# A planner's order of instructions, and a region that keeps it

## Chip, core and metric

The kernel runs on one core of one Trainium2 chip. A core has a matrix engine (TensorE; PE for its matmuls, PEld for its weight loads), a vector engine (VectorE, DVE), a scalar engine (ScalarE, ACT), a general engine (GpSimd, POOL) and SyncE (SP), which issues the DMAs here. Each engine takes its instructions from a list of its own and waits on semaphores for what others make. The metric is the device time of one execution in microseconds (us); less is better.

## What is computed

Four graph layers run over 16 graphs of 1024 nodes with 128 features. Cut to what matters:

```
x = layernorm(x + relu((mask^T x) U / deg))                       # layer 0: sum over neighbours
x = layernorm(x + softmax(clip(q k^T * adj) - 9e15*(1-adj)) v)    # layer 1: attention, q, k, v = relu(x W + b)
x = layernorm(x + concat_h softmax_i(leaky(s_i + s_j)) (x W)_h)   # layer 2: four heads, masked by adj
x = layernorm(x + sage3(x, dilate(adj)))                          # layer 3: three sage layers on thinned edges
```

`dilate` walks the rows of a graph and drops every n-th neighbour of a row, and earlier drops change later rows; the kernel replaces the walk by two rounds of thresholds and counts.

## The kernel before

Two stages follow one another. `fuse` (L181) computes layers 0 to 2 and the dilation for all graphs; `sage` (L1070) computes layer 3. The change touches the last statement of `fuse` alone.

In `fuse` a graph is a batch `b`. The work of a batch is cut into ten generators, called sequences: `loads` (the rows of adj come by DMA), `signs` (`has` on DVE at L332, `over` on ACT at L336), `dilate`, `layer0`, `layer1`, `scores`, `values`, `sides`, `layer2` and `layer2_sums`. Each yields a `Step` before the instructions that it issues: the engine, a cost in us that the planner books, the marks that it waits for, and the buffers that it takes and gives back.

`Loom.run` (L163) is a planner that runs while the program is being made. It keeps a clock for each engine from the booked costs. Over and over it takes the step that can start first, and among those of the same engine that can start within 0.1 us of it the one that is due first by a table of phases; it books that step and lets its sequence emit the instructions. So the order in which the kernel emits its instructions, over all engines, is the order of planned start. For every hand-over from one engine to another it books 0.3 us, and 0.5 us when the receiver is PE.

What the planner computes is not yet the order on the engines. The framework that builds the program has a scheduler of its own. It uses the order of emission as priorities, runs its own model of time, and lets an instruction pass an earlier one on the same engine when the earlier one is not ready in that model. The instructions of the built program carry running numbers in the order of emission, and they can be set against the trace: in the ten batches between 591.2 and 2076.0 us, 1101 of 3001 DVE instructions, 717 of 1664 ACT instructions and 1146 of 11732 matmuls ran ahead of one on their engine that had been emitted earlier.

Steps that the prediction follows, in the order of emission within a batch:

- `stays` (L537): 16 blocks of nine matmuls into `ps_n` (L541, L544, L547), two PSUM buffers; each is emptied by ACT into `adt` (L557). The last block is the last reader of the tile `ranked`, which has one buffer.
- norm 2 and norm 0 (`Norm.apply`, L576): 17 small DVE instructions on the tile `ln_t` (L582 to L594), nearly each reading the one before, then eight on ACT (L599). The planner books 1.9 us for the DVE part.
- the scans (L354): eight DVE instructions that fill `ranked` of the next batch, booked at 2.2 us each.
- `weights`: `top` (L879, DVE), `ps_top` (L882, PE), `peak` and `peaks` (L885, L887, DVE), `ps_cap` (L890, PE), `cap` (L896, DVE), `ac` (L899, DVE; L903, L904, ACT), `wh` (L893, ACT).
- `pieces`: `src` (L917, L921, DVE), then three parts of it rounded in turn on ACT (L924, L930) and DVE (L927, L933).
- `ps_m` (L968, PE): 192 matmuls that read `pieces`; `every` (L973, ACT) empties it.
- `sides`: `sg` (L818, ACT, 32 a batch) and `g` (L827, DVE), which the matmuls `ps_b` (L998) read.
- `values`: transposes (L605, PE), `pt` (L772, ACT), `ps_a` (L779, PE). `ps_s` of the scores is L744 and L748.

Of the kernel before, what the change touches and what calls it, by code (L numbers as in the profile page):

```python
# [180 lines left out]
def fuse(S, ctx, a, x3, adt_d, viol, B=16):  # L181
# [20 lines left out]
    tc, nc = S.tc, S.nc  # L202
# [111 lines left out]
    def signs(batches):  # L314

        for k, c in enumerate(batches):
            yield k, "signs"
            again = k == len(batches) - 1
            if k >= 2:
                yield Step(  # L320
                    None, 0.0, after=(f"m {k - 2} 1", f"sides {k - 2}") + ((f"dilated {k - 2}",) if k > 2 else ())
                )
            links[c] = p2.tile([P, 8, EDGE + N], F8, name="has")
            V.memset(links[c][:, :, EDGE - 2 : EDGE].bitcast(I16), 0)
            has[c] = links[c][:, :, EDGE:]
            for r in range(8):
                yield Step(
                    "DVE", 0.64, after=(f"a {k} {r}",), give=[("a", r)] if again else (),
                    mark=f"has {k} {r}",
                )  # L330
                t = raw.pop((k, r))
                V.tensor_scalar(has[c][:, r, :], t, 0.0, LINK, ALU.not_equal, ALU.mult, saturate=False)  # L332
                if not again:
                    yield Step("ACT", 1.13, after=(f"a {k} {r}",), take=[("over", (k, r))], give=[("a", r)])
                    over[c, r] = p2.tile([P, N], F8, name="over", bufs=OVER)
                    nc.scalar.activation(  # L336
                        over[c, r], t, AF.Sign, bias=under, accum_out=cut[:, c, r : r + 1], saturate=False
                    )
# [351 lines left out]
    def layer1():  # L690
        for b in each:
            yield b, "keys"
            yield Step(None, 0.0, after=(f"x1 {b} 1",) + ((f"early {b - 1}",) if b else ()))
            yield from keys(b)
# [35 lines left out]
    def scores():  # L730
        for b in each:
            yield b, "scores"
            yield Step(None, 0.0, after=(f"q {b}", f"k {b}"))
            qt, kt, _ = qkv[b]
            low = lows[b] = sm.tile([P, 8], F32, name="low")
            for ib in range(8):
                for f in range(0, N, 512):
                    yield Step(
                        "PE", 1.07, after=(), take=() if f else [("two", "s"), ("pr", ib)],
                        give=[("over", (b, ib))] if f else (),  # L740
                    )
                    if f == 0:
                        ps_s = two.tile([P, N], F32, name="ps_s", tag="two")
                    nc.tensor.matmul(  # L744
                        ps_s[:, f : f + 512], qt[:, ib * P : (ib + 1) * P], kt[:, f : f + 512],
                        start=True, stop=False,
                    )
                    nc.tensor.matmul(  # L748
                        ps_s[:, f : f + 512], shut, over[b, ib][:, f : f + 512], start=False, stop=True
                    )  # L750
                yield Step("DVE", 1.15)
                V.tensor_reduce(low[:, ib : ib + 1], ps_s, AX.X, ALU.min)  # L752
                yield Step("ACT", 1.1, give=[("two", "s")], mark=f"pr {b} {ib}")
                pr, tot = p2.tile([P, N], F32, name="pr"), sm.tile([P, 1], F32, name="tot")
                nc.scalar.activation(pr, ps_s, AF.Exp, bias=low[:, ib : ib + 1], scale=-1.0, accum_out=tot)  # L755
                made[b, ib] = pr, tot
# [46 lines left out]
    def sides():  # L803

        for b in range(B):
            yield b, "sides"
            for h in range(H):
                for q in range(4):
                    for k in range(2):
                        yield Step(  # L810
                            "ACT", 1.04, after=(f"row {b} {h}", f"st {b}"),
                            take=[("g", (b, h, q // 2))] if k == 0 and q % 2 == 0 else (), mark=f"sg {b} {h} {q}",
                        )
                        st, side = stuff[b][0:2]
                        if k == 0:
                            sg = p2.tile([P, 2, N], I8, name="sg")
                        ib = 2 * q + k
                        nc.scalar.activation(  # L818
                            sg[:, k, :], rows[b, h], AF.Sign, bias=st[:, 1, h, ib : ib + 1], scale=-1.0
                        )  # L820
                    if q == 3 and h + 2 < H:
                        yield Step("SP", 0.2, lag=2.5, mark=f"row {b} {h + 2}")
                        row(b, h + 2)
                    yield Step("DVE", 0.6, after=(f"sg {b} {h} {q}",), mark=f"g {b} {h} {q // 2}" if q % 2 else None)
                    if q % 2 == 0:
                        side[h, q // 2] = p4.tile([P, 4, N], F8, name="g")
                    V.tensor_tensor(  # L827
                        side[h, q // 2][:, q % 2 * 2 : q % 2 * 2 + 2, :].bitcast(I16), sg.bitcast(I16),
                        has[b][:, 2 * q : 2 * q + 2, :].bitcast(I16), ALU.bitwise_and,
                    )  # L830
            yield Step(None, 0.0, mark=f"sides {b}")

    def layer2():
        for b in each:
            yield b, "weights"
            yield Step(None, 0.0, after=(f"x2 {b} 1",) + ((f"raw wh {b - 1}", f"sides {b - 1}") if b else ()))
            yield from weights(b)
# [110 lines left out]
    def layer2_sums():  # L948
        for b in each:
            yield b, "sums"  # L950
            yield from outputs(b)

    def outputs(b):
# [73 lines left out]
        for c in range(8):  # L1027
# [7 lines left out]
    loom = Loom(  # L1035
        155.0, 0.1,
        {
            "loads": (364.0, 3.34),
            "signs": (813.0, 0.64),
            "ranks": (991.0, 0.88),  # L1040
            "match": (-250.0, 0.22),
            "round 0": (-892.0, 0.48),
            "round 1": (-332.0, 0.32),
# [17 lines left out]
        },  # L1061
        two=2, one=2, dps=2, g=4, pr=2, a=2, w2k=4, over=OVER,
    )
    loom.run(
        layer2_sums(), sides(), values(), layer2(), scores(), layer1(), layer0(), signs(batches),
        loads(batches), dilate(batches),
    )
# [292 lines left out]
def tile_gnn_stack(tc, a, out):  # L1360

    nc = tc.nc
    with ExitStack() as outer:
        flag = outer.enter_context(tc.tile_pool(name="flag", bufs=1))
        viol = flag.tile([P, 8], F32, name="viol")
        nc.vector.memset(viol, 0.0)
        with ExitStack() as ctx:  # L1370
            S = Setup(ctx, tc)
            dram = ctx.enter_context(tc.tile_pool(name="fast_dram", bufs=1, space=DRAM))
            x3 = dram.tile([16, 8 * P, P], F32, name="x3")
            adt_d = dram.tile([16, 8, P, 8 * P], F8, name="adt_d")
            with ExitStack() as first:
                fuse(S, first, a, x3, adt_d, viol)
            with ExitStack() as third:
                layers = [[a[f"L3_gnn_{n}{i}"] for n in ("Wr", "Wx", "b", "g", "be")] for i in (1, 2, 3)]
                sage(S, third, x3, a["nodemask"], adt_d, viol, layers, a["L3_gnn_Wl"], a["L3_gnn_bl"], out)
            todo = flag.tile([1, 1], I32, name="todo")  # L1380
            with tc.tile_pool(name="flag_ps", bufs=1, space=PSUM) as fp:
                ps = fp.tile([1, 8], F32, name="ps_flag")
                nc.tensor.matmul(ps, S.ones[:, 0:1], viol, start=True, stop=True)
                total = flag.tile([1, 1], F32, name="total")
                nc.vector.tensor_reduce(total, ps, mybir.AxisListType.X, ALU.max)
                nc.vector.tensor_copy(todo, total)
        v = nc.values_load(todo[0:1, 0:1], min_val=0, max_val=16384)  # L1387
        with tc.If(v > 0):
            general(tc, a, out)
# [676 lines left out]
```

## Time and profile before

| what | us |
|---|---|
| median of 3 runs | 3487.2 (3486.0 to 3496.1) |
| the profiled execution, as timed | 3491.4 |
| its span, first to last instruction | 3489.7 |
| PE busy in the span | 3010.6 (86%) |
| DVE busy | 2595.9 (74%) |
| ACT busy | 2323.7 (67%) |
| x3 stores of batches 2 and 12 issued at | 591.2 and 2076.0 |

The profile gives the busy time of each engine, groups of equal instructions, and the idle time before them with what ended it. `L998 PE ps_b` stands for line 998, engine PE, output tile `ps_b`. The stores of x3 are the end of a batch in `fuse`: ten batches lie between 591.2 and 2076.0 us, so a batch takes 148.5 us. `fuse` ends at about 2461 us, where the last x3 is stored; the rest is `sage`. In the ten batches PE is busy for 1308.7 us, ACT for 1190.8 and DVE for 1125.5.

### The profile page before, as it was taken

Reading aid. Unit: us, or ns where it says so; the run is one execution under the profiler, and the core shown is the slowest. Engines: PE = TensorE matmul, PEld = TensorE weight load, DVE = VectorE, ACT = ScalarE, POOL = GpSimd, SP = SyncE. Lnnn points to the kernel's source line nnn. Section 1 sums busy time; section 2 is a strip of 40 time slices with the busy share of each in tenths; the row PEclk is TensorE's granted clock in tenths of the full one; section 3 lists DMA queues with packets and bytes.
Section 4 is the critical chain, followed back from the end, with each engine's and each line's share of the span. In section 5 each row is a group of like instructions: output and inputs, shape, how many; then the busy total and the mean of one; then the engine's idle time right before and its main releaser. Section 6 shows DMA issues by size and latency. Waiting matters only on the chain. (4 is left out here: it accounts for less than half of the span.)

```text
span 3489.7 us, 66022 instructions
## 1 busy us (share of the span) xinstructions
PE 3010.6 (86%) x25972; PEld 2377.9 (68%) x25972; DVE 2595.9 (74%) x7057; ACT 2323.7 (67%) x4149; POOL 2.0 (0%) x10
## 2 busy tenths in 40 slices
PE   4897988989898898988989889896599899989974
PEld 3676777777777777767777777775366666666653
DVE  4657687777868778687776868768388788888865
ACT  3786878878778787787878878777355444433334
POOL 0000000000000000000000000000000000000000
PEclk8898989989999999999989999998799999999987
DMA  4121112021120211202111120211333222212224
GB/s 109 37 67 37 61 44 92 25 80 51 48 86 25 80 56 50 77 22 92 49 56 57 42 92 25 74 42 39 76 101 91 73 61 61 61 49 61 61 88 122
DMA packets 224447, 219.97 MB, mean 63 GB/s; under 512 B 48000, under 2 KB 198528, under 8 KB 224128
## 3 DMA queue, kind: packets, MB, share of 16 engines
q1 hardware_dynamic: 224128, 215.67, 20.1%
q8 instruction: 205, 3.36, 0.4%
q14 instruction: 114, 0.93, 0.1%
HBM read 181.80 MB, written 33.82 MB: 62 GB/s over the span
## 5 line engine op out<-in xcount | busy, mean ns | idle before, releaser
L818 ACT ACTIVATE sg<-row,st 128x1024 int8<-128x1024 f32 x512 | 564.0, 1141 | 75.0 <-DVE g L827 55.7
L1165 PE MATMUL ps_g<-pz,ad 128*128 128x384 bf16 (+1 forms) x3072 | 535.8, 327 | 4.6 <-DMA ad<-adt_d 4.4
L1165 PEld LDWEIGHTS <-ad 128*128 128x128 fp8e4 x3072 | 297.6, 98 | 203.8 <-DMA ad<-adt_d 16.6
L998 PE MATMUL ps_b<-pieces,g 128*128 128x198 bf16 x4096 | 392.9, 249 | 3.8 <-DVE g L827 3.1
L998 PEld LDWEIGHTS <-g 128*128 128x128 fp8e4 x4096 | 354.6, 96 | 9.9 <-DVE g L827 4.6
L1182 ACT ACTIVATE sq<-xw 128x128 f32<-128x128 f32 x384 | 117.7, 307 | 305.7 <-DVE xw L1175 272.2
L779 PE MATMUL ps_a<-vn,pt 128*128 128x128 f32 x2048 | 272.7, 283 | 32.6 <-ACT pt L772 32.6
L426 ACT ACTIVATE x<-both,thr 128x1024 f16<-128x1024 bf16 (+7 forms) x384 | 276.1, 769 | 31.6 <-DVE thr L412 22.7
L744 PE MATMUL ps_s<-kt,qt 128*128 128x512 f32 x512 | 276.4, 622 | 24.0 <-ACT pr L755 14.5
L354 DVE TENSOR_TENSOR_SCAN ranked<-has 128x1024 bf16<-128x1024 fp8e4 x128 | 286.8, 2272 | 12.0 <-PE ps_n L547 11.9
L968 PE MATMUL ps_m<-pieces,has 128*128 128x132 bf16 x3072 | 224.7, 240 | 75.4 <-ACT pieces L930 45.0
L779 PEld LDWEIGHTS ps_a<-vn,pt 128*128 128x128 f32 x2048 | 248.6, 193 | 52.5 <-ACT pt L772 40.0
L968 PEld LDWEIGHTS <-has 128*128 128x128 fp8e4 x3072 | 217.7, 106 | 84.8 <-issue 84.4
L656 PE MATMUL ps_g<-py,has 128*128 128x128 bf16 (+1 forms) x3072 | 227.4, 241 | 35.8 <-DVE cap L896 30.6
L656 PEld LDWEIGHTS <-has 128*128 128x128 fp8e4 x3072 | 215.7, 109 | 37.5 <-issue 32.1
L557 ACT ACTIVATE adt<-ps_n 128x512 fp8e4<-128x512 f32 x256 | 146.5, 592 | 101.8 <-PE ps_n L547 92.8
L1174 DVE TENSOR_REDUCE t<-ps_g 128x128 f32<-128x384 f32 x384 | 206.2, 546 | 6.4 <-PE ps_g L1165 6.2
L1121 PE MATMUL ps_z<-wzx,raw 128*128 128x256 f32 x768 | 192.1, 393 | 10.7 <-ACT raw L1196 3.9
L752 DVE TENSOR_REDUCE low<-ps_s 128x1 f32<-128x1024 f32 x128 | 156.3, 1221 | 52.5 <-PE ps_s L748 48.5
L827 DVE TENSOR_TENSOR g<-sg,has 128x1024 int16<-128x1024 int16 x256 | 173.4, 679 | 28.4 <-ACT sg L818 27.5
L336 ACT ACTIVATE over<-a,under 128x1024 fp8e4<-128x1024 f32 x128 | 147.3, 1151 | 50.4 <-DMA a<-in_adj_dram 43.0
L1121 PEld LDWEIGHTS ps_z<-wzx,raw 128*128 128x128 f32 x768 | 144.1, 195 | 45.9 <-PE ps_y L1142 13.6
(255 smaller groups left out, 5928.8 us busy)
## 6 DMA issues: line engine op xcount, KB each, us to landing
a<-in_adj_dram SPq DMA_DIRECT2D x136, 512.0 KB, 3.7
ad<-adt_d SPq DMA_DIRECT2D x384, 128.0 KB, 2.3
row<-t_d SPq DMA_DIRECT2D x64, 512.0 KB, 3.8
adt_d<-adt SPq DMA_DIRECT2D x128, 128.0 KB, 1.7
xn<-x SPq DMA_DIRECT2D x32, 512.0 KB, 4.2
x<-in_x_dram SPq DMA_DIRECT2D x16, 512.0 KB, 5.4
x<-x SPq DMA_DIRECT2D x16, 512.0 KB, 4.2
out_dram<-y SPq DMA_DIRECT2D x16, 512.0 KB, 3.2
```

The source lines that it names most:

```text
L354: V.tensor_tensor_scan(ranked[c][:, r, :], has[c][:, r, :], links[c][:, r, EDGE - 1 : EDGE - 1 + N].bitcast(U8), 0.0, ALU.add, ALU.subtract,)
L426: nc.scalar.activation(x, both[:, at[r] : at[r + 1]], AF.Abs, bias=far[:, r : r + 1], scale=2.0)
L656: nc.tensor.matmul(ps_g[:, k, 0:e], has[b][:, jb, ib * P : (ib + 1) * P], py[:, jb, q * P : q * P + e], start=(jb == 0 and q == 2), stop=( ...
L744: nc.tensor.matmul(ps_s[:, f : f + 512], qt[:, ib * P : (ib + 1) * P], kt[:, f : f + 512], start=True, stop=False,)
L779: nc.tensor.matmul(ps_a[:, 0:P], pt[:, c * P : (c + 1) * P], vn[:, c, :], start=(c == 0), stop=(c == 7))
L818: nc.scalar.activation(sg[:, k, :], rows[b, h], AF.Sign, bias=st[:, 1, h, ib : ib + 1], scale=-1.0)
L827: V.tensor_tensor(side[h, q // 2][:, q % 2 * 2 : q % 2 * 2 + 2, :].bitcast(I16), sg.bitcast(I16), has[b][:, 2 * q : 2 * q + 2, :].bitcast( ...
L968: nc.tensor.matmul(ps_m[:, u // 2, o : o + H * D1], has[b][:, ib, jb * P : (jb + 1) * P], pieces[:, ib, 1, :, t, :], start=(t == 0 and ib ...
L998: nc.tensor.matmul(ps_b[:, u // 2, (u % 2) * 2 * W3 : (u % 2 + 1) * 2 * W3], side[h, q][:, k, jb * P : (jb + 1) * P], pieces[:, 4 * q + k, ...
L1121: nc.tensor.matmul(ps_z[:, k, :], raw[:, b, c * P : (c + 1) * P], wzx, start=True, stop=True)
L1165: nc.tensor.matmul(ps_g[:, 0:width], adt[jb][:, ib * P : (ib + 1) * P], pz[:, jb, 0:width], start=(jb == 0), stop=(jb == 7),)
L1174: nc.vector.tensor_reduce(t, ps_g[:, 0 : 3 * P].rearrange("p (t d) -> p d t", t=3), AX.X, ALU.add)
```

## The change

```diff
-    loom.run(
+    with tc.manual_schedule(): loom.run(
         layer2_sums(), sides(), values(), layer2(), scores(), layer1(), layer0(), signs(batches),
         loads(batches), dilate(batches),
     )
```

Inside the region the framework's scheduler keeps, on each engine and on SP's queue of DMA issues, the order in which the instructions were emitted. No instruction is added or removed, no buffer changes, and the planner's table is as it was. The instructions of `fuse` ahead of the last statement (constants, weights) and all of `sage` are ordered as before.

## The prediction

> **What bounds the kernel.** The change acts in `fuse` alone, so I read the page's 40 slices first: `fuse` fills the first 28, and no engine is full in all of them.
>
> ```profile
> ## 2 busy tenths in 40 slices
> PE   4897988989898898988989889896599899989974
> DVE  4657687777868778687776868768388788888865
> ACT  3786878878778787787878878777355444433334
> ```
>
> PE is the fullest, at eight or nine tenths. The page's chain of waits names only the last ACT instruction, so it says nothing of `fuse`. From the x3 stores ten batches take 1484.8 us, 148.5 each. In them PE is busy for 1308.7 us: 130.9 a batch, so 17.6 us of idle time a batch is all that an order can win. Windows of 10 us through one batch show where that lies (PE, PEld, DVE, ACT, POOL busy with counts, granted clock, DMA share, GB/s).
>
> ```profile
> 1170.00:1180.00 10.00, 9.98 (x132) 8.88 (x130) 8.69 (x38) 6.21 (x14) 0.00 (x0) 1.00 0.16 52
> 1180.00:1190.00 10.00, 9.76 (x142) 8.97 (x139) 5.16 (x7) 8.28 (x18) 0.00 (x0) 1.00 0.62 199
> 1190.00:1200.00 10.00, 2.72 (x31) 2.55 (x29) 10.00 (x11) 6.69 (x8) 0.00 (x0) 0.69 0.19 58
> 1200.00:1210.00 10.00, 5.50 (x50) 5.04 (x49) 10.00 (x24) 8.72 (x12) 0.00 (x0) 0.67 0.15 52
> 1210.00:1220.00 10.00, 10.00 (x137) 10.00 (x136) 10.00 (x29) 5.61 (x8) 0.00 (x0) 0.79 0.01 2
> ```
>
> From 1190 to 1210 PE is idle for 11.8 us and DVE for none; everywhere else in the batch PE has nine tenths or more, but for two windows. So a batch is bound by PE, with one **gap of some 12 us that DVE sets**. The waits of the ten batches agree: PE waits 48.0 us for `peaks`, 23.6 for `cap`, 45.9 for `pieces` (32.5, 9.8 and 3.6), together 11.8 a batch. The rest is small: 24.6 us for `pt`, 10.0 for `pr`, 7.4 for `sums`, 3.8 for `part`.
>
> **What the change moves.** It adds no instruction; every edit is an order. I set the running numbers of emission against the trace and walk one batch.
>
> *What goes.* The framework's scheduler fills the short pauses between dependent DVE instructions with long ones. Norm 0 of this batch, in the DVE timeline:
>
> ```profile
> 1212.37 0.15 DVE L585 TENSOR_TENSOR ln_t<-ln_t 128x8 f32<-128x8 f32 x1
> 1212.44 2.27 DVE L354 TENSOR_TENSOR_SCAN ranked<-has 128x1024 bf16<-128x1024 fp8e4 x1
> 1214.65 0.13 DVE L586 TENSOR_SCALAR ln_t<-ln_t 128x8 f32<-128x8 f32 x1
> 1214.70 2.27 DVE L354 TENSOR_TENSOR_SCAN ranked<-has 128x1024 bf16<-128x1024 fp8e4 x1
> 1216.90 0.13 DVE L588 TENSOR_SCALAR ln_t<-ln_t 128x8 int32<-128x8 int32 x1
> ```
>
> It runs from 1211.28 to 1220.95, 9.7 us; norm 1, which nothing interrupts, takes 3.0 (1163.66 to 1166.69). On ACT whole `sg` of 1.14 us run ahead of `pt`, `pr` and `xt`. What that costs is only what PE waits for: half of the waits for `pt` and `pr` ((24.6 + 10.0)/20 = 1.7 us a batch: one `sg` or less stood in front, and the rest is PE's own transposes or DVE), and those for `sums` and `part`, (7.4 + 3.8)/10 = 1.1. **Gain 2.8 us a batch.** Ends: 0 if each only moves to the next producer, 4.6 if all of it goes.
>
> *What comes, in the gap.* ACT's order in the trace at the `stays`:
>
> ```profile
> 1178.20 1.31 ACT L557 ACTIVATE adt<-ps_n 128x512 fp8e4<-128x512 f32 x2 [1.73 <-PE ps_n L547]
> 1179.93 3.19 ACT L599 ACTIVATE x<-x,ln_t 128x128 f32<-128x128 f32 x8 [0.43 <-DVE ln_t L594]
> ```
>
> The emitted order has four L599 of norm 2, then one L557, four L599, one L557. The planner could put them first because it books 1.9 us for the norm that takes 3.0. In the kept order: the last statistic ends at 1175.4, the norm at 1178.5, four L599 at 0.39 end at 1180.05, and the L557 that ran at 1178.20 ends at 1180.55. Queued behind it on ACT is everything else, and PE's twelfth block of `ps_n` needs the buffer: it starts at 1180.7 and not at 1178.85. The thirteenth waits for the next four L599 and its L557, until 1182.7. Blocks of 0.66 and the 12 `ps_g` between them (0.7 each dozen) bring the last block to 1186.8; in the trace it ended at 1185.9. The scans of the next batch wait for it: 0.9 us later.
>
> Then DVE alone. In the trace, scans start at 1186.02; `peaks` is done at 1195.77, `cap` at 1198.68, `ac` (after one more scan) at 1200.96, and the first half of `pieces` (L933) at 1209.64. Kept order: three scans of 2.2 from 1187.0 to 1193.7; `top` (which ran early, at 1178.0) 1193.9; L671 and two L574, 0.7; a scan, 1196.8; `peak`, `peaks` 1197.2; two `g` and L663, 1.3; a scan, 1200.7; `cap`, `ac`, 1201.0, as in the trace. But `wh` ran early on ACT, at 1191.95; now it is queued behind two `sg` that wait for the `g` at 1197.8, and two L667, so it ends at 1201.4 and the exponentials at 1201.8. `src` takes 2.7 on DVE, to 1204.9; L663 and `g` 0.7; the scan that ran before `ac` now stands here, 2.2; the first L927 half is done at 1208.9, its ACT cast at 1210, L933 at 1212.2. So PE gets `pieces` **2.5 us later**. In the trace PE had also done 8 `ps_t` and 4 `ps_f` (0.61 and 0.70 us by their rows, about 0.9 together without the pipeline's end) that the kept order leaves for later. **Loss 3.4 us a batch**; ends 0, if the walk's waits overlap better, and 6, if the clock adds to it.
>
> Here a rule speaks. PE's timeline in the gap:
>
> ```profile
> 1195.82 0.59 PE L890 MATMUL ps_cap<-peaks,ones 8*128 8x8 f32 x2 [4.95 <-DVE peaks L887]
> 1198.74 5.31 PE L656 MATMUL ps_g<-py,has 128*128 128x129 bf16 x48 [2.33 <-DVE cap L896]
> 1208.39 0.38 PE L968 MATMUL ps_m<-pieces,has 128*128 128x132 bf16 x2 [3.25 <-ACT pieces L930]
> 1209.69 6.48 PE L968 MATMUL ps_m<-pieces,has 128*128 128x132 bf16 x71 [0.92 <-DVE pieces L933]
> ```
>
> 48 matmuls take 5.31 us; in the 1.00 windows a dozen takes 0.7, so they would take 2.8. The Trainium skill (TensorE: Matmul & The Clock Gate, "HAM oscillation") says that a pause longer than about 3.4 us sends the clock to half. The walk cuts the pause of 4.95 into 1.9, 1.3, 2.1, 2.4 and 3.3, so by the rule the clock would stay full, and `ps_m`, half-speed from 1209.7 to 1214, would be 2.0 us shorter: loss 1.4 and not 3.4. By the row the clock is 0.67 in a window in which PE was busy for 5.5 of 10 us with no pause over 3.25. I take the row.
>
> *What comes, elsewhere.* Where PE ran ahead of a matmul that was not ready, the kept order waits. By running numbers that is 2.9 us of matmuls a batch between `values` and the counts (`ps_a` ahead of L452 1.75, L452, L491 and L495 ahead of `ps_a` 0.9, L491 ahead of L452 0.2). A third would be ready sooner without the swaps on ACT and DVE: **loss 1.9 us** (0 to 2.9). On ACT 36 us a batch ran ahead of an unready instruction, 22 of it `sg`; its cover is slack, since the `g` of 1114.52 was read at 1162.59, and ACT has 29.4 us of idle time a batch. On SP the order of the loads, rows and stores returns to emission; `has` still lands ahead of `ps_g` (the last load at about 1167, `ps_g` at 1169): nothing, and up to 2 us if a store of `adt` blocks a load.
>
> **The sum.** 3.4 + 1.9 - 2.8 = 2.5 us a batch, in 15 batches (the first and last are thin and count 0): 37. The profiled execution of 3491.4 becomes 3528; it lies 4.2 above the median, so the median becomes **3524**, 1.1% slower.
>
> **The rivals.**
>
> *Faster, 3420.* One mechanism: norm 2 ends before the L557 are due. If the last `ps_n` ends before 1185.0, the scans start a microsecond earlier instead of later, `pieces` comes at 1209 and the clock stays full. Per batch -0.5 for the gap, -2.0 for the clock, -2.8 for the swaps, +0.8 for unready matmuls: -4.5, times 15 = -67. For it: the planner books scans, `sg` and `g` as the trace spaces them (2.2, 1.04, 0.6), and DVE's swaps are many. Against it: the booked 1.9 for the norm, and a PE that is already nine tenths full outside the gap.
>
> *Much slower, 3612.* ACT becomes the bound. The 36 us that ran ahead find no later place because each head waits (`every` for `ps_m`, `xt` for its transposes, the round's L426 for its thresholds). With 119.1 us busy, ACT bounds the batch once its waits pass 29.4. At 157 us a batch: +8.3 x 15 = +125. Against it: `g` has tens of microseconds of slack.
>
> *No change.* The gains and losses are near each other, or the region binds less than it says: 3487.
>
> **Chances.** A measurement of this kernel can tell 0.3%, about 10 us, from no change. Forecast (3498 to 3570) 0.42; much slower 0.17; faster 0.33; no change 0.08. So slower 0.59, same 0.08, faster 0.33. The range that leaves out two in ten is 3415 to 3630; the forecast's own range is 3498 to 3570.
>
> **What would show it.** DVE: L582 to L594 without a scan between, in about 3 us. ACT: L557 and L599 alternating one to four, and PE waiting for `adt` in `stays` where it had 3.4 us in ten batches. Fewer waits for `pt` and `sums`. The stretch from the last `ps_n` to the first L933, 23.7 us in the trace, near 25. I am wrong if the batch is shorter than 148.5, above all if the granted clock stays at 1.00 through the gap.

## The result, and the profile after

The changed kernel takes **3571.5 us** (median of 4 runs, 3561.7 to 3572.8) against 3486.6 (3478.9 to 3496.1) on the same chip: ratio 1.0236, interval 1.0212 to 1.0259. It is 85 us slower; the forecast was slower by 37. The profiled run took 3572.8 us, its span 3571.1.

One correction to the table ahead of the prediction: 591.2 and 2076.0 are the times at which the x3 stores of batches 2 and 12 landed. They were issued at 586.6 and 2070.2. From here on all stores are counted at their issue (L1032).

| between x3 stores, us | before | after | difference |
|---|---|---|---|
| start to store of batch 2 | 586.6 | 592.0 | +5.4 |
| ten batches, to the store of 12 | 1483.6 | 1522.1 | +38.5 (3.85 a batch) |
| 12 to 13 | 145.7 | 152.4 | +6.7 |
| 13 to 15 | 241.9 | 273.3 | +31.4 |
| the rest, `sage` | 1031.9 | 1031.3 | -0.6 |

So all of it is in `fuse`, and nearly half of it (38 of 82) in the last three batches, to which the forecast gave 5 at most.

In the ten batches PE is busy for 130.8 us a batch, as before (130.7). Nothing was added to its work or to the time that work takes; the whole loss is time in which PE waits. The largest waits of PE in those ten batches, before (us in total, times, longest):

```profile
PE ps_cap L890 <- DVE peaks L887: 48.0, 10, 5.0
PE ps_m L968 <- ACT pieces L930: 32.5, 10, 3.3
PE ps_a L779 <- ACT pt L772: 24.6, 20, 2.5
PE ps_g L656 <- DVE cap L896: 23.6, 10, 2.7
PE ps_m L968 <- DVE pieces L933: 9.8, 10, 1.5
PE ps_n L541 <- ACT adt L557: 3.7, 16, 0.4
```

and after:

```profile
PE ps_m L968 <- ACT pieces L930: 52.6, 10, 5.3
PE ps_n L541 <- ACT adt L557: 35.8, 20, 4.0
PE ps_g L656 <- DVE cap L896: 29.7, 10, 3.1
PE ps_cap L890 <- DVE peaks L887: 24.3, 10, 2.4
PE ps_top L882 <- DVE top L879: 17.8, 10, 1.8
PE ps_m L968 <- DVE pieces L933: 17.8, 10, 1.8
PE ps_a L779 <- ACT pt L772: 10.1, 20, 0.6
PE ps_s L452 <- DVE part L441: 10.0, 20, 0.9
PE ps_s L744 <- ACT pr L755: 6.8, 10, 0.7
```

New is the second row after: 3.6 us a batch for a free `ps_n` buffer (0.4 before). From the first to the last matmul of the `stays` it is now 24.9 us on average where it was 22.2, though 260 matmuls stand in that stretch and not 284. `pieces` has grown from 4.6 to 7.0 a batch, `top` from nothing to 1.8; `peaks` has shrunk from 4.8 to 2.4, `pt` from 2.5 to 1.0. The place in ACT's timeline, for the batch whose gap the prediction walked through:

```profile
1197.38 1.65 ACT L599 ACTIVATE x<-x,ln_t 128x128 f32<-128x128 f32 x4 [2.81 <-DVE ln_t L594]
1198.93 0.57 ACT L557 ACTIVATE adt<-ps_n 128x512 fp8e4<-128x512 f32 x1
1199.40 1.64 ACT L599 ACTIVATE x<-x,ln_t 128x128 f32<-128x128 f32 x4
1200.94 0.58 ACT L557 ACTIVATE adt<-ps_n 128x512 fp8e4<-128x512 f32 x1
```

It is the order of the walk: four L599, one L557, four, one. Ahead of the first, ACT does nothing for 2.81 us, because its head is an L599 whose norm isn't ready; the L557 behind it could have run. PE pays:

```profile
1199.55 0.45 PE L541 MATMUL ps_n<-ranked,less 128*128 128x512 bf16 x1 [2.63 <-ACT adt L557]
...
1201.57 0.58 PE L541 MATMUL ps_n<-ranked,less 128*128 128x512 bf16 x1 [0.72 <-ACT adt L557]
...
1216.98 0.59 PE L890 MATMUL ps_cap<-peaks,ones 8*128 8x8 f32 x2 [2.43 <-DVE peaks L887]
1220.50 4.33 PE L656 MATMUL ps_g<-py,has 128*128 128x129 bf16 x48 [2.92 <-DVE cap L896]
...
1230.17 0.27 PE L968 MATMUL ps_m<-pieces,has 128*128 128x132 bf16 x1 [5.26 <-ACT pieces L930]
```

And the windows of 10 us through this gap (PE, PEld, DVE, ACT, POOL busy with counts, granted clock, DMA share, GB/s):

```profile
1198.00:1208.00 10.00, 7.73 (x96) 6.72 (x96) 2.59 (x6) 6.90 (x16) 0.00 (x0) 0.83 0.39 126
1208.00:1218.00 10.00, 5.37 (x67) 5.02 (x67) 9.93 (x14) 5.21 (x7) 0.00 (x0) 0.94 0.25 88
1218.00:1228.00 10.00, 4.41 (x49) 4.29 (x49) 9.93 (x20) 9.97 (x15) 0.00 (x0) 0.67 0.31 91
1228.00:1238.00 10.00, 6.05 (x60) 5.88 (x60) 8.54 (x29) 2.68 (x4) 0.00 (x0) 0.54 0.05 16
```

In the first window DVE has 2.59 us of work, because its scans wait for the last `ps_n` (38.0 us in ten batches, 4.9 before). In the next two it is full. A stall on ACT has become a pause on DVE just ahead of the stretch that DVE sets.

### The profile page after: what moved, and what is told of

The parts are those of the page before. It is cut to its first block, busy times and chain, and to the rows that moved or that the text cites. A ratio compares the mean times of both kernels' runs of the same rounds, so it can differ in the third digit from the quotient of the medians.

```text
span 3571.1 us, 66293 instructions
## 1 busy us (share of the span) xinstructions
PE 3020.9 (85%) x25972; PEld 2397.1 (67%) x25972; DVE 2657.6 (74%) x7057; ACT 2319.1 (65%) x4149; POOL 2.0 (0%) x10
## 5 line engine op out<-in xcount | busy, mean ns | idle before, releaser
L818 ACT ACTIVATE sg<-row,st 128x1024 int8<-128x1024 f32 x512 | 564.2, 1142 | 33.2 <-DVE g L827 24.7
L1165 PE MATMUL ps_g<-pz,ad 128*128 128x384 bf16 (+1 forms) x3072 | 534.8, 328 | 2.6 <-DMA ad<-adt_d 2.6
L1165 PEld LDWEIGHTS <-ad 128*128 128x128 fp8e4 x3072 | 297.7, 98 | 200.7 <-DMA ad<-adt_d 13.4
L998 PE MATMUL ps_b<-pieces,g 128*128 128x198 bf16 x4096 | 395.5, 250 | 5.0 <-DVE g L827 4.8
L998 PEld LDWEIGHTS <-g 128*128 128x128 fp8e4 x4096 | 354.4, 96 | 11.3 <-DVE g L827 6.7
L968 PEld LDWEIGHTS <-has 128*128 128x128 fp8e4 x3072 | 223.0, 108 | 115.7 <-issue 115.5
L744 PE MATMUL ps_s<-kt,qt 128*128 128x512 f32 x512 | 276.3, 622 | 19.5 <-ACT pr L755 14.7
L779 PE MATMUL ps_a<-vn,pt 128*128 128x128 f32 x2048 | 275.4, 284 | 19.5 <-ACT pt L772 19.5
L779 PEld LDWEIGHTS ps_a<-vn,pt 128*128 128x128 f32 x2048 | 248.2, 194 | 36.1 <-ACT pt L772 28.7
L656 PEld LDWEIGHTS <-has 128*128 128x128 fp8e4 x3072 | 218.7, 110 | 48.6 <-issue 45.0
L557 ACT ACTIVATE adt<-ps_n 128x512 fp8e4<-128x512 f32 x256 | 147.9, 591 | 81.2 <-PE ps_n L547 63.9
L599 ACT ACTIVATE x<-x,ln_t 128x128 f32<-128x128 f32 x384 | 155.9, 483 | 58.0 <-DVE ln_t L594 58.0
```

The lines of the kernel that those rows point to most:

```text
L656: nc.tensor.matmul(ps_g[:, k, 0:e], has[b][:, jb, ib * P : (ib + 1) * P], py[:, jb, q * P : q * P + e], start=(jb == 0 and q == 2), stop=( ...
L744: nc.tensor.matmul(ps_s[:, f : f + 512], qt[:, ib * P : (ib + 1) * P], kt[:, f : f + 512], start=True, stop=False,)
L779: nc.tensor.matmul(ps_a[:, 0:P], pt[:, c * P : (c + 1) * P], vn[:, c, :], start=(c == 0), stop=(c == 7))
L818: nc.scalar.activation(sg[:, k, :], rows[b, h], AF.Sign, bias=st[:, 1, h, ib : ib + 1], scale=-1.0)
L968: nc.tensor.matmul(ps_m[:, u // 2, o : o + H * D1], has[b][:, ib, jb * P : (jb + 1) * P], pieces[:, ib, 1, :, t, :], start=(t == 0 and ib ...
L998: nc.tensor.matmul(ps_b[:, u // 2, (u % 2) * 2 * W3 : (u % 2 + 1) * 2 * W3], side[h, q][:, k, jb * P : (jb + 1) * P], pieces[:, 4 * q + k, ...
```

## The experiments

Theory A: ACT's kept order at this one place is the cause. Its rivals: another engine's kept order is (P, D and S for PE, DVE and SP); the planner's durations are wrong (M); the table of phases fits the framework's re-ordering at one point, so that every displaced order costs (F). Further rivals (B, B', G, H) are named where their runs were planned. All results:

| run | us | ratio to before, interval | a batch (ten) | 13 to 15 |
|---|---|---|---|---|
| e1_act: order held on ACT alone | 3578.6 | 1.0264 (1.0244 to 1.0284) | 153.7 | 259.2 |
| e1_pe: on PE alone | 3568.6 | 1.0229 (1.0210 to 1.0248) | 153.1 | 253.0 |
| e1_dve: on DVE alone | 3530.9 | 1.0126 (1.0103 to 1.0149) | 150.4 | 258.2 |
| e1_sp: on SP and POOL alone | 3534.6 | 1.0127 (1.0100 to 1.0154) | 152.6 | 242.6 |
| e2_head: all, until batch 12 is stored | 3536.4 | 1.0131 (1.0107 to 1.0155) | 152.5 | 238.5 |
| e2_tail: all, from then on | 3529.9 | 1.0105 (1.0081 to 1.0128) | 148.2 | 268.9 |
| e2_book_held: all, norm booked at 3.05 | 3543.3 | 1.0142 (1.0118 to 1.0165) | 149.9* | 267.9 |
| e2_book_free: none, norm booked at 3.05 | 3512.6 | 1.0052 (1.0026 to 1.0077) | 150.2* | 254.0 |
| e3_jog_free: none, window 0.2 | 3572.8 | 1.0242 (1.0218 to 1.0265) | 154.1 | 250.9 |
| e3_norm_late: all, L599 behind the stays | 3447.3 | 0.9883 (0.9864 to 0.9903) | 143.7 | 266.3 |
| e3_scan_late: all, sixth scan behind L927 | 3619.4 | 1.0378 (1.0357 to 1.0399) | 157.6 | 270.4 |
| e3_both_late: both of these | 3566.0 | 1.0217 (1.0193 to 1.0242) | 154.2 | 271.1 |
| e4_norm_free: none, L599 behind the stays | 3479.4 | 0.9968 (0.9957 to 0.9979) | 147.7 | 236.8 |
| e4_norm_act: ACT alone, L599 behind the stays | 3490.9 | 1.0004 (0.9994 to 1.0014) | 147.7 | 257.8 |
| e4_norm_head: until 12, L599 behind the stays | 3437.2 | 0.9852 (0.9830 to 0.9874) | 143.8 | 238.1 |

\* from the store of batch 4 to that of 12, where the batches are even; before has 148.1 there and after 152.4.

The last column goes by the stores of x3. Where the L599 are moved and ACT's order is held to the end, the last store itself comes later, and the column with it; the end of this section has these batches by PE's work.

### One engine's order at a time

```diff
-    with tc.manual_schedule(): loom.run(
+    with tc.manual_schedule(engines={mybir.EngineType.Activation}): loom.run(
```

and the same with DVE, with PE, and with SP and Pool. The named engine then has the changed kernel's order; the others are ordered by the scheduler around it.

> The region holds the order on ACT alone; PE, DVE and SP are left to the framework's scheduler. Theory A (the cost is ACT's head of line: four L599 of norm 2 stand in front of an L557 whose ps_n is long ready, so PE runs out of ps_n buffers in stays, once in each batch, and the pieces come late): 3540 to 3575 us, and PE waiting at L541 for adt L557 some 3 us a batch. Rival P (the cost is PE's kept order, a matmul that isn't ready in front of one that is): within 20 us of before. Rival D (the cost is DVE's kept order): within 20 us of before.

> The region holds the order on DVE alone. Theory A: 3470 to 3510 us, since the 17 instructions of norm 2 run without scans between them (3.0 us as against 5.9 in the batches before), which ends ACT's wait earlier. Rival D: 3540 us or more. Rival P: within 20 us of before.

> The region holds the order on PE alone. Theory A: 3490 to 3520 us (PE heads that aren't ready cost some 1.9 us a batch). Rival P: 3540 us or more, most of the 85 us, with the long tail of the last batches in it. Rival D: within 20 us of before.

> The region holds the order on SP and POOL alone, so that the loads and stores keep the order in which they are emitted and nothing else does. Theories A, P and D: within 15 us of before. A fourth theory, S (a store that waits for its data stands in front of the loads of a later batch): 3540 us or more, with PE or ACT waiting for has at the starts of batches.

No theory came through whole. ACT alone costs 90 us, 4 more than the range of A, but PE's wait at L541 is only 1.0 us a batch and not 3: the loss shows at `pieces` (8.1 a batch, 4.6 before). PE alone costs 81, as P said, though with little of the tail that P expected (253.0 us), and even the queue of loads and stores alone 47. A missed all of its other three ranges. D and S came within 10 us of theirs, but not by the wait that S named: PE's only wait for a load is 1.9 us a batch for x. The four sum to some 260 us where all together cost 85, so these losses are not parts of a sum. What they share is where PE waits: for the chain of `top`, `peaks`, `cap` and `pieces` it waits 14 to 16 us a batch in each of them, and 12 before. It seems that each engine's order is worth something only against the orders of the others; no run separates this further.

### The last batches, and the booked time of the norm

For the first two, the region is left, or entered, in `Loom.run` where the step marked `stored 12` has been emitted:

```diff
+            s.done, mark = self.emit(s.step, start), s.step.mark
+            s.advance(self.period); mark == "stored 12" and self.held.close()
...
+    loom.held = ExitStack(); loom.held.enter_context(tc.manual_schedule()); loom.run(
```

> All engines in emission order until batch 12 is stored; what is emitted behind that is left to the scheduler. If the 31 us that the changed kernel loses between the stores of batches 13 and 15 belong to the kept order of the last batches themselves: 3525 to 3545 us, and 242 to 252 us between these stores. If they are left over from the batches before (work that the head leaves undone): 3560 us or more, and some 270 us between these stores.

> The reverse: scheduler until batch 12 is stored, emission order behind it. If the loss of the last batches is their own order's: 3510 to 3530 us with 265 to 275 us between the stores of batches 13 and 15, and ten batches of 1484 us as before. If it is left over from the batches before: within 12 us of before.

The two parts are separate causes. Held until batch 12, the kernel loses 1.31% and its last batches take 238.5 us, as before; held from there on, it loses 1.05%, its ten batches take 148.2 us a batch, as before, and the last ones 268.9. The sum, 2.36%, is the loss of the whole. So the 31 us at the end are the order of the last batches themselves and not work left over.

The other two book what the trace shows for the norm, once with and once without the region:

```diff
-            yield Step("DVE", 1.9)
+            yield Step("DVE", 3.05)
             t = sm.tile([P, 6, 8, 1], F32, name="ln_t")
```

> All engines in emission order as in the changed kernel, but the planner books 3.05 us, and not 1.9, for the 17 small DVE instructions of each norm. Theory M (the kept order costs where the planner's durations are wrong, and norm 2 is the wrong one in the stays): PE's wait at L541 for adt L557 falls from 3.6 us a batch to under 1, and the time from 3571 to 3515 to 3540 us. Rival F (the table of phases was fitted with the framework's re-ordering at work, so that every displaced order costs, whatever its durations): 3555 us or more, the wait only found elsewhere, at pieces or cap.

> The same booking of 3.05 us without the region: the framework's scheduler re-orders as before. Theory M: within 15 us of before, because the scheduler passes over what isn't ready and the booking sets little. Rival F: 20 us or more slower, since this also displaces the order that the phases were fitted to.

With the region ACT no longer waits for `ln_t` (from 900 to 2100 us of the trace 21.0 us after, none here), and the kernel gains 0.9%, 2.5 us a batch. But PE's wait for `adt` only falls from 3.5 to 2.9 us a batch, where M expected less than 1, so M's picture is half right: the L557 now stand behind L599 that run (1.64 us for four), and no longer behind one that is stuck. Without the region the same edit costs 17 us (0.5%), which is F's sign, but lies between what M (up to 15) and F (20 or more) expected.

### The L599 out of the stays

This edit moves eight L599 a batch and changes what the planner arranges behind them. They wait, in the planner's model, for the step that ends the stays:

```diff
-        def apply(self, mark):
+        def apply(self, mark, late=()):
...
-                yield Step("ACT", 1.55, mark=f"{mark} {q}")
+                yield Step("ACT", 1.55, after=(None, *late), mark=f"{mark} {q}")
...
-        yield from norm.apply(f"x3 {b}")
+        yield from norm.apply(f"x3 {b}", (f"dilated {b + 1}",))
```

> Region as in the changed kernel, but the planner gives the eight L599 of norm 2 only behind the last L557 of the stays that they stood between. Theory A (PE's 3.6 us a batch at L541 for adt L557 are what the kept order adds, and they come from the L599 in front of the L557): this wait falls under 1 us a batch, the last ps_n comes 2 to 3 us sooner, and the batch goes from 152.2 to 149.0 to 150.5: 3525 to 3550 us. Rival B (DVE sets the gap whatever the stays do; the wait only moves to peaks, cap or pieces): 3560 us or more.

It beats the expectation: 3447 us, 1.2% under the kernel *before*. ACT's timeline at the end of the stays:

```profile
1158.30 1.21 ACT L557 ACTIVATE adt<-ps_n 128x512 fp8e4<-128x512 f32 x2 [0.67 <-ACT adt L557]
1160.31 1.21 ACT L557 ACTIVATE adt<-ps_n 128x512 fp8e4<-128x512 f32 x2 [0.79 <-PE ps_n L547]
1161.41 3.17 ACT L599 ACTIVATE x<-x,ln_t 128x128 f32<-128x128 f32 x8
```

All eight L599 now run where no L557 of these stays stands behind them. PE's largest waits in ten batches:

```profile
PE ps_m L968 <- ACT pieces L930: 37.4, 10, 4.4
PE ps_top L882 <- DVE top L879: 36.6, 10, 3.7
PE ps_cap L890 <- DVE peaks L887: 23.3, 10, 2.4
PE ps_m L968 <- DVE pieces L933: 18.0, 10, 1.8
```

Against the changed kernel, a batch is 8.5 us shorter: `adt` 3.5, `cap` 3.0, `pieces` 1.5, less 1.9 for `top` and 0.6 for `y`; and PE's own busy time falls from 130.8 to 127.9 for the same 1296 matmuls a batch. Its clock is at half for 14.0 us a batch in place of 23.8. In that time PE is busy for 8.7 us in place of 14.6. If a matmul then takes twice as long, as the prediction's rows have it (5.31 us for 48, 2.8 at full clock), half of the 5.9 us between them is what the slower clock adds: by this estimate 2.9 us, all of the fall. Rival B falls: the stays set when the scans start, and so the gap.

Not all of the 8.5 us is the place of the L599 itself. From the first to the last matmul of the stays it is 20.2 us in place of 24.9, for the same 260 matmuls: 4.7. From there to the start of L933 it is 22.1 in place of 24.7: 2.6 more. In that second stretch the planner has also put other work in another order; `wh` starts 7.4 us behind the last `ps_n` and not 13.6. No run separates the two.

The scan in front of the first L927 was moved in the same manner:

```diff
-            yield Step("DVE", 2.2, after=(f"has {k} {r}",))
+            yield Step("DVE", 2.2, after=(f"has {k} {r}", *((f"rest {k - 1} 1",) if r == 5 and k > 2 else ())))
```

> Region as in the changed kernel, but the sixth scan of a batch (L354), which the kept order puts in front of the first L927, is given behind both L927. Theory A: the wait for pieces L930 falls from 5.3 to some 3.1 us a batch as in the kernel before, and the batch by 1.5 to 2.2 us: 3540 to 3555 us. Rival B' (the scan takes the same time wherever it stands, and the ranks come as much later as the pieces come sooner): 3565 us or more.

> Both of these in one kernel. Theory A: the gains add, 147.0 to 148.8 us a batch and 3500 to 3525 us, the rest above before being the last batches. Rivals B and B': no more than the better of the two alone.

Both miss. The edit makes the plan uneven: batches of 130 to 189 us follow each other. In the ten batches `pieces` L930 costs only 1.2 us a batch, but PE now waits in many other places (L744 for `pr` 2.0, L779 for `pt` 1.8, L452 for `part` 1.7) and is busy for 134 us a batch. Combined with the moved L599 it loses what these gain. What the scan's place alone is worth stays open, since the plan did not stay otherwise as it was.

### What the kernel before is worth as a reference

```diff
-        155.0, 0.1,
+        155.0, 0.2,
```

> No region: the kernel before with one number of the planner moved, the window in which the due times decide, from 0.1 to 0.2 us. Theory F (the table of phases fits the framework's re-ordering at one point only, and any displacement costs): 3505 us or more, by waits in the same gap. Rival (the scheduler absorbs small displacements, and only holding an order costs): within 12 us of before.

One number of the planner, moved by 0.1 us with no region anywhere, costs 85 us: as much as the change. So a large part of what the kernel before has seems to be that its table fits the orders which come out of this planner and this scheduler together; one other value was tried, and no more. The loss isn't where F looked for it: PE's largest new waits are 4.8 us a batch at L605 for `x` of L599 and 2.5 at L368 for `both`, outside of the gap, and PE is busy for 134 us a batch. F is right about the size of what displaced orders can cost here, and wrong that all of them cost:

> The moved L599 without the region. Theory A (with the L599 moved, the emitted order is the better one, and the framework's re-ordering now only costs): 3470 to 3495 us, PE waiting for peaks, pt and pieces as in the kernel before, since there no L599 stood in front of an L557. Rival G (the gain of 40 us is that of the moved L599 alone, the region takes no part in it): 3440 to 3455 us.

> The moved L599 with the order held on ACT alone, which cost 90 us without the move. Theory A (that loss was the L599 in front of the L557): 3450 to 3500 us. Rival H (holding one engine alone costs because the others are then ordered for times that don't come, whatever ACT's order is): 3540 us or more.

> The moved L599 with the region until batch 12 is stored, the rest left to the scheduler. If the kept order of the last batches costs by itself, as its own part of the loss did: 3410 to 3430 us, some 242 us between the stores of batches 13 and 15 in place of 266. If the moved L599 has removed it too: 3440 to 3455 us.

Without the region the moved L599 gain 11 us; with it they turn +85 into -40, so G falls. With order held on ACT alone they remove all of its 90 us, though PE, DVE and SP are still left to the scheduler: A has the cause of that loss right, and H falls. The way it takes there is another than A said, since PE hardly waited at L541 in e1_act. So **the region itself isn't what costs**: with the L599 out of the stays it gains 0.85% over the scheduler (3447 us against 3479). In the run without it, PE's waits for `peaks` and `pt` in ten batches are:

```profile
PE ps_cap L890 <- DVE peaks L887: 78.2, 10, 7.8
PE ps_a L779 <- ACT pt L772: 23.8, 20, 2.2
```

against 23.3 and 10.1 with it. The wait for `pt` is one of the swaps that the forecast wanted undone. For the first, the region has another wait in exchange, 36.6 for `top`.

Leaving the region before the last batches gives the best kernel of all, 3437 us, 1.5% under the one before, between the two results that were expected. By the stores its last batches are 28 us shorter than those of e3_norm_late, but the time is only 10 less. The stores mislead here: the L599 of the last batch wait for the last stays, so that its x3 is stored 36.6 us behind PE's last L998 of that batch (20.3 in the changed kernel, 19.1 in e4_norm_head), and nothing is lost by that: `sage` has its first L1165 75.3 us behind this L998, and 74.3 in e4_norm_head. From the last L998 of batch 13 to that of batch 15, the windows are (PE, PEld, DVE, ACT, POOL busy with counts, granted clock, DMA share, GB/s; before, after, e3_norm_late):

```profile
2201.00:2440.00 239.00, 188.79 (x1985) 159.67 (x1985) 184.55 (x473) 178.15 (x255) 0.00 (x0) 0.89 0.14 45
2252.00:2519.50 267.50, 198.75 (x1983) 168.91 (x1983) 193.32 (x481) 179.75 (x260) 0.00 (x0) 0.84 0.13 44
2148.60:2398.00 249.40, 189.23 (x1984) 159.40 (x1982) 192.09 (x479) 179.02 (x257) 0.00 (x0) 0.88 0.14 47
```

The change adds 28.5 us there, for the same matmuls, and moving the L599 takes 18.1 of them away. The 10.4 that are left go when the region is left: 236.2 us in e4_norm_head.

## Why the prediction was right and wrong

**The bound** was read rightly: PE nine tenths full, and one gap that DVE sets. In the ten batches PE's busy time moved by 0.1 us a batch between the two kernels, and every microsecond lost is a wait.

**The gain for undone swaps**, 2.8 us a batch. Measured: `pt` 1.45, `pr` 0.3 and `sums` at L605 0.75 gained, `part` 0.6 lost: 1.9. Right in kind, a third too large. (The `part` stand at L452, where the forecast had PE wait for its heads; booked there, the gain is 2.5.)

**PE's heads that aren't ready**, 1.9. Measured: `qt` 0.4 and `both` 0.2 more: 0.6, or 1.2 with `part`. Too large. Other small waits fell by 0.4.

**The gap**, 3.4: this step was mis-sized. Measured: `adt` +3.2, `top` +1.7, `cap` +0.6, `pieces` +2.5, `peaks` -2.4: 5.6. The walk had the order of ACT in the stays right to the instruction, and from the last `ps_n` (1206.6) to the end of the first half of L933 (1232.2) it takes 25.6 us, where it said near 25. What it had wrong was the stays themselves. It let the last block of `ps_n` come 0.9 us later, because blocks and the `ps_g` between them would make up the rest; PE waited 3.6 us a batch for `adt` there, and the stays became 2.7 us longer. With the L599 out of the way this wait is 0.1, the stays are 4.7 us shorter, and the batch with what follows 8.5.

**The ends**, counted 0. This is the step that failed most. Of the 48 us by which the forecast was short, at least 26 are the last two batches (+31.4, where 2.5 a batch would be 5). It took the end for thin, with nothing to lose. There PE is busy for 186 of 242 us before, and 200 of 273 after. In the gap of the last batch, before:

```profile
2361.00:2385.00 24.00, 4.43 (x42) 3.55 (x41) 22.48 (x26) 17.00 (x25) 0.00 (x0) 0.65 0.26 87
```

and after:

```profile
2431.00:2458.00 27.00, 5.04 (x35) 4.22 (x35) 26.93 (x28) 16.65 (x19) 0.00 (x0) 0.56 0.13 47
```

DVE is full in both, and no next batch fills PE. e2_tail shows that it is the kept order there that costs. The L599 have their part in it (PE's waits for `adt` there are 0.4 us before, 7.8 after and 1.5 in e3_norm_late), but they don't make the end worse than the middle. By PE's last L998 the two batches take 239.0 us before, 267.5 after and 249.4 in e3_norm_late: moving the L599 takes 18 of the 28.5 us away, about as much for each of the two as in the middle (8.5). Against the kernel before, the two then still lose 10 us, where two in the middle gain 9. This rest of some 20 us is what the forecast missed most; the largest wait that stays in it is for `part` at L452 (2.5 us before, 11.2 after, 7.6 with the L599 moved). Which instructions of the last batches cause it was not settled.

**The clock.** The prediction weighed the rule of the Trainium skill (TensorE: Matmul & The Clock Gate, "HAM oscillation": half clock after a pause of over some 3.4 us) against the row, and took the row. The row was right: in the gap after, the clock was 0.83, 0.94, 0.67 and 0.54, and it went to half at 1199.7, behind a pause of 2.63 us. (The walk's pauses were all shorter than the rule's limit. In the changed kernel the one of 5.26 us for `pieces` is not, so the rule would not have kept the whole gap at full clock.) The rule would have made the forecast 30 us smaller (2.0 a batch less, 15 times) and so worse.

**The rivals.** "Much slower", ACT as the bound at 157 us a batch, did not come: ACT is busy for 118.8 us a batch, as before. "Faster" is the instructive one. Its mechanism was that norm 2 ends before the L557 are due; it gave -4.5 us a batch and 3420 us. In the changed kernel its condition isn't met. e3_norm_late comes to the same by another way, with the L599 behind the L557, and there the batch is 4.7 us shorter than before. Its terms come out near the forecast's: the gap -0.6 (forecast -0.5), PE's busy time, for the clock, -2.8 (-2.0), the swaps -1.9 (-2.8), unready matmuls +1.0 (+0.8), other small waits -0.4. The time is 3447 and not 3420, because the gain is that of the batches in the middle: up to the last L998 of batch 2 it is 2 us, and from batch 13 to 15 the kernel loses 10.

## What to carry to other kernels

Before an order is fixed, look for the instruction at the head of a queue whose producer the plan has booked too short, and for what stands behind it: here eight activations stood in front of one that frees a buffer of the fullest engine, and moving them, with what the planner re-arranged behind them, turned 2.4% lost into 1.2% gained. A fixed order is only as good as the plan that it fixes, and these runs suggest that a plan that was fitted with a re-ordering scheduler behind it is no longer the same plan without it. Count the last batches by themselves: a stall there has no next batch to hide it. And count them by the work of the fullest engine: a store can come later without anything being lost.

## What the hardware showed that was not expected

The granted clock of PE changes on a fixed grid. In the trace of before all 57 stretches at half clock begin at whole multiples of 3.413 us from each other, and all but the last are whole multiples of that long (most of them 3.41, 6.83 or 10.24 us). What PE did in one window of this grid goes with the clock in the next: of some 115 windows in which PE was busy for less than half of the time, some 93% were followed by half clock; of some 860 in which it was busy for seven tenths or more, 98% were followed by the full one. After: some 90% of 147, and 98% of 857. The grid is the free-running window of 3413 ns of the Trainium skill (TensorE: Matmul & The Clock Gate, "Part 1: The HAM clock gate"); the page has the clock fall after an idle window. In these traces no pause of a whole window is needed: in the changed kernel one of 2.63 us stood ahead of the half clock at 1199.7, and one of 2.43 us ahead of that at 1216.8, in windows in which PE was busy for 23% and 28%.

Small dependent VectorE instructions cost more than their durations. In the 17 of a norm one starts 0.20 us after the one that it needs, and 0.08 after one that it doesn't; 17 of them take 3.05 us, and not the booked 1.9.
